# Staging a layer's input in free slots of another operand's tile, and an earlier PSUM read in V

## The chip, the cores and the metric

One core of a Trainium2 chip runs the whole program. The metric is device time in microseconds, the median of three runs. TensorE (PE; its weight loads stand as PEld), VectorE (DVE), ScalarE (ACT), GpSimd (POOL) and the DMA queue of SyncE (SP) work side by side; each engine takes its instructions in order.

## The reference

128 graphs of 128 nodes with 512 features share one adjacency matrix. Layer 0 is a graph convolution, layer 1 attention with 8 heads under the mask of the adjacency; both are pre-normalised and have a residual.

```
h = relu(layernorm(x));  x = x + norm_adj @ (h @ W0) + b0
h = relu(layernorm(x));  q, k, v = h @ Wq + bq, h @ Wk + bk, h @ Wv + bv
attn = softmax(q @ k.T / 8 + (1 - adj) * -1e9)      # 8 heads of 64
x = x + (attn @ v) @ Wo + bo
```

All is float32; x is 128 x 128 x 512.

## The kernel before

The 128 graphs go in 32 groups of four. A group's x stands in two xt tiles (half 0 and half 1, two graphs each, 128 x 1024 float32, 512 KB); the pool has 8 such tiles, so four groups' worth. All five 512 x 512 products of a group are done by a Winograd-like scheme of seven block products P1 to P7; most of these are cut again in the same way. For that an operand tile has 40 slots of 128 x 128: the four blocks A11, A12, S1, A22 (slots 0 to 15), the combinations S2, S3, S4 (16 to 27), and inner combinations (28 to 39). `Operands.combine` (L370) makes the combinations, for most groups on GpSimd: four instructions of 128 x 512 (L373 to L376), then nine of 128 x 256 (L94). There are three such tiles: op_mix (its profile name is op_a) for the graph convolution, op_norm (op_h) for the normalised input of q, k, v, and op_att (op_o) for the output projection.

The program is one software pipeline over slots t. Slot t has five stages, each of seven steps 0 to 6 (a product each): W is the graph convolution's weight product of group t + 1, Q, K and V are q, k, v of group t, and Y is the output projection of group t - 1. `block` (L1092) runs a stage: at each step it first issues whatever is planned for that place, then the step's matmuls and first reads (`step`), then, at the place with a "b", its later reads (`rest`). A place with a "c" comes after both. The list `at(t, place, f, ...)` (L975 and after) is the order written out by hand; no scheduler changes it.

What the later parts speak of, in a slot t:

- `load_x` of group t + 2 at W2 (half 0) and W5 (half 1), from SyncE's queue, L170. It writes an xt tile that held group t - 2, whose `store_half` was issued at the end of Y of slot t - 1 (half 0) or at W3 of slot t (half 1), L903.
- `ln1` (statistics at L325, `bn_stats` on VectorE) at Q0b, Q1b and Q3b; the scale rs and shift nb on GpSimd (L331, L333); `gcn_norm` on ScalarE (L344) at Q3 to Q6; `gcn_mix` on TensorE (bank pa) and ScalarE (L662); `gcn_operands` (op_a) on GpSimd at K2.
- `gcn_residual` adds the bias b0 in place to xt on GpSimd (L348, 128 x 1024) at Y1 and Y2. W of the next slot then adds its products to that xt.
- `norm_h` of group t + 1 on ScalarE (L344) at K6, K6, V0b, V1; `split_h` (L745, 128 x 1024 words in halves) at V0, V0, V1b, V2; `write_h` (L748, DMA to planes_h) at V1b and V2b; `turn_h` (L754, a DMA transpose into op_h) at V5 and Y1b; `attention_operands` (op_h) on GpSimd at Y5.
- the end of attention for group t - 1, in W, Q and K: `softmax_end` (L854, GpSimd), `split_att` (L859, ScalarE; L860, DMA to planes), `turn_att` (L863, DMA transpose), four of each, one per graph b. `attend` (L885, banks po, b and a) reads the result at V0, then `output_operands` combines op_o on GpSimd.
- weights are reloaded from DRAM in four parts (`reload_w`, L1072; 704 KB, the last 448 KB). Into V's buffer go the graph convolution's weights for the next slot: part 0 at V3, part 1 (slots 22 to 32) at Y0, part 2 (slots 11 to 21) at Y1, part 3 at Y3.

In V the seven products write banks a, d0/d1, b and c. V1 fills banks d; ScalarE's copy (L790) moves d0's columns to v, and VectorE (L440) then adds the other parts of d to v; V4 accumulates into banks d again.

Of the kernel before, what the change touches and what calls it, by code (L numbers as in the profile page):

```python
# [8 lines left out]
F32 = mybir.dt.float32  # L9
# [3 lines left out]
ALU = mybir.AluOpType  # L13
# [14 lines left out]
A11, A12, S1, A22, S2, S3, S4 = range(7)  # L28
# [17 lines left out]
LEFT_AT = {A11: 0, A12: 4, S1: 8, A22: 12, S2: 16, S3: 20, S4: 24}  # L46
# [51 lines left out]
def kernel(  # L98
# [16 lines left out]
    nc = tc.nc  # L115
    B, N, D = x.shape
    P = 128
# [10 lines left out]
    xp = ctx.enter_context(tc.tile_pool(name="xp", bufs=8))  # L128
# [32 lines left out]
    ones = att_buf[4][:, NC, :]  # L161
    nc.sync.dma_start(adj_sb, adj)

    xts = {}

    def load_x(g, halves=(0, 1)):
        for half in halves:
            t = xts[g, half] = xp.tile([P, 2, D], F32, tag="xt", name=f"xt_{g}_{half}")
            b = g * GB + 2 * half
            nc.sync.dma_start(t, x[b : b + 2].rearrange("b n f -> n b f"))  # L170

# [30 lines left out]
    def load_b(name, b):  # L202
        t = const.tile([P, D], F32, name=f"b_{name}")
        nc.sync.dma_start(t, b.partition_broadcast(P))
        return t

    xts[0, 0] = xp.tile([P, 2, D], F32, tag="xt", name="xt_0_0")
    for b in range(2):
        nc.sync.dma_start(xts[0, 0][:, b, :], x[b])
    load_w("0", w0, w_buf[0])  # L210
    load_x(0, (1,))
    b0_bc = load_b("0", b0)
    load_x(1)
    load_w("q", wq, w_buf[1])
    bqk = const.tile([P, 2, NC], F32, name="bqk")
# [6 lines left out]
    with nc.allow_non_contiguous_dma(reason="one bias vector, once"):  # L222
        nc.sync.dma_start(bv_c, bv.rearrange("(c p) -> p c", p=P))
    load_x(2)


# [8 lines left out]
    def constants():  # L235
        nc.vector.memset(mhalf, -0.5)
        nc.vector.memset(ones, 1.0)

        nc.scalar.activation(warm, mhalf[:, 0:1], AF.Exp)
        make_identity(nc, ident)  # L240
        nc.gpsimd.tensor_copy(ident16, ident)

        deg = const.tile([P, 1], F32, name="deg")
        nc.vector.tensor_reduce(deg, adj_sb, AX.X, ALU.add)
        degc = const.tile([P, 1], F32, name="degc")
        nc.vector.tensor_scalar(degc, deg, 1.1754944e-38, None, ALU.max)
        dis = const.tile([P, 1], F32, name="dis")
        nc.gpsimd.tensor_tensor(dis, degc, mhalf[:, 0:1], ALU.pow)
        pos = const.tile([P, 1], F32, name="pos")
        nc.vector.tensor_scalar(pos, deg, 0.0, None, ALU.is_gt)  # L250

        nc.vector.tensor_scalar(msk, adj_sb, 1.0, NEG, ALU.subtract, ALU.mult)
        ln1(0, 0, (0,))
        ln1(0, 0, (1,))
        disz = const.tile([P, 1], F32, name="disz")
        nc.vector.tensor_tensor(disz, dis, pos, ALU.mult)
        nc.vector.tensor_scalar(an, adj_sb, disz, None, ALU.mult)
        gcn_norm(0, 0)
        gcn_norm(0, 1)
        spin(9)  # L260
        pt_an = small_bank("pt_an")
        nc.tensor.transpose(pt_an[:, :N], an, ident)
        nc.vector.tensor_scalar(ant, pt_an[:, :N], disz, None, ALU.mult)
# [73 lines left out]
    def normalised(src, j, norm, name, start=False):  # L337
        rs, nb = norm.rs, norm.nb
        if start:

            h = third
        else:
            h = hp.tile([P, D], F32, tag="h", name=name)
        nc.scalar.activation(h, src[:, j, :], AF.Relu, bias=nb[:, j : j + 1], scale=rs[:, j : j + 1])  # L344
        return h

    def add_bias(t, bias):
        nc.gpsimd.tensor_tensor(t, t, bias.unsqueeze(1).to_broadcast([P, t.shape[1], D]), ALU.add)  # L348

# [32 lines left out]
    op_mix, op_norm, op_att = (Operands(f"op_{k}") for k in "aho")  # L384
# [249 lines left out]
    scale1, op_a, op_h, op_o = {}, {}, {}, {}  # L634
    hs = {}

    def ln1(g, half, js=(0, 1), ready=None):

        if (g, half) not in scale1:
            scale1[g, half] = Norm(xts[g, half], f"1_{g}_{half}")  # L640
        for j in js:
            scale1[g, half].statistics(j)
        if ready is None or ready:
            scale1[g, half].scale(ready or js)

    def gcn_norm(g, b):
        half, j = divmod(b, 2)
        hs[g, b] = normalised(xts[g, half], j, scale1[g, half], f"h_{g}_{b}", g == 1 and b == 2)

    def gcn_mix(g, b):  # L650
        if b == 0:
# [14 lines left out]

    def gcn_residual(g, half, js=(0, 1)):

        add_bias(xts[g, half][:, js[0] : js[-1] + 1, :], b0_bc)

    def residual_projection(g, a, w, inner):
        def region(half, y):
# [86 lines left out]
    def attention_residual(g, half):  # L759
        add_bias(xts[g, half], bo_bc)  # L760
# [149 lines left out]
    def at(slot, place, f, *args):  # L910
        plan.setdefault((slot, place), []).append((f, *args))

    for t in range(-1, NG + 1):
# [3 lines left out]
        if 0 <= t - 1 < NG - 1:  # L917
            g = t - 1
# [27 lines left out]
        if t == 0:  # L946

            at(0, "Q0b", ln2, 1, 0)
            at(0, "Q1b", ln2, 1, 1)
            at(0, "K6", norm_h, 1, 0)  # L950
            at(0, "K6", norm_h, 1, 1)
            at(1, "W0", transpose_h, 1, 0)
            at(1, "W0", norm_h, 1, 2)
            at(1, "W1", transpose_h, 1, 1)
            at(1, "W1", norm_h, 1, 3)
            at(1, "W2", transpose_h, 1, 2)
            at(1, "W3", transpose_h, 1, 3)
            at(1, "W4b", attention_operands, 1)
            at(2, "Q5", attention_residual, 1, 0)
            at(2, "K1", attention_residual, 1, 1)  # L960
        elif 1 <= t + 1 < NG and t >= 0:
            g = t + 1
            at(t, "K0b" if g < NG - 1 else "Q0b", ln2, g, 0)
            at(t, "K6b" if g < NG - 1 else "Q3b", ln2, g, 1)
            if g == NG - 1:

                places = ("Q3", "Q4", "Q5", "Q5", "Q6", "Q6", "K1", "K2", "K2")
                steps = ((norm_h, 0), (norm_h, 1), (transpose_h, 0), (norm_h, 2), (transpose_h, 1), (norm_h, 3))
                steps += ((transpose_h, 2), (transpose_h, 3))
            else:  # L970
                places = ("K6", "K6", "V0b", "V1", "V1b", "V2", None, None, "Y5")
                steps = ((norm_h, 0), (norm_h, 1), (norm_h, 2), (norm_h, 3), (split_h, 2), (split_h, 3))
                for half in range(2):
                    at(t, ("V1b", "V2b")[half], write_h, g, half)
                    at(t, ("V5", "Y1b")[half], turn_h, g, half)  # L975
            for place, (f, b) in zip(places, steps):
                at(t, place, f, g, b)
            at(t, places[8], attention_operands, g)
            at(t + 1, "Q3", attention_residual, g, 0)
            at(t + 1, "Q4", attention_residual, g, 1)  # L980
# [1 line left out]

            at(t, "Y3" if t == NG else "Q3" if last else "W3", store_half, t - 2, 1)
        if 3 <= t + 2 < NG:
            at(t, "W2" if t > 1 else "W0", load_x, t + 2, (0,))
            at(t, "W5" if t > 1 else "W0", load_x, t + 2, (1,))
        if 2 <= t + 2 < NG:
            g = t + 2
            if t > 0:
                at(t, "Q0b", ln1, g, 0, (0,), ())  # L990
                at(t, "Q1b", ln1, g, 0, (1,), (0, 1))
                at(t, "Q3b", ln1, g, 1)
            places = (("Q3", "Q5"), ("Q4", "Q6"), ("Q5b", "K1"), ("Q6", "K2"))
            for b, (norm, mix) in enumerate(places):
                at(t, norm, gcn_norm, g, b)
                at(t, mix, gcn_mix, g, b)
            at(t, "K2" if t > 0 else "V1b", gcn_operands, g)
            at(t, "Y1" if t > 0 else "K3", gcn_residual, g, 0)
            at(t, "Y2" if t > 0 else "K3", gcn_residual, g, 1)
        if 0 <= t < NG:  # L1000
            g = t
            for b in (0, 1, 3, 2):
# [31 lines left out]
        if last:  # L1034
            g = t
# [38 lines left out]
    def reloads_of(t):  # L1074

        when = {
            "W": ((t, "W6"), (t, "K3"), (t, "Q1"), (t, "K3")),
            "Q": ((t, "K4"), (t, "K6"), (t, "V0"), (t, "V1")),
            "V": ((t, "V3"), (t, "Y0"), (t, "Y1"), (t, "Y3")),
            "Y": ((t, "Y5"), (t + 1, "W0"), (t + 1, "W0"), (t + 1, "W3" if t + 1 < NG - 1 else "Q5")),  # L1080
        }
        if t == 1:

            when["Q"] = ((1, "K3"),) * 4
        for kind in "WQVY":
            if kind == "W" and t + 1 == NG or kind in "QV" and t == NG:
                continue
            reading[0] += 1
            for part, place in enumerate(when[kind]):
                at(*place, reload_w, reading[0] + 2, part)  # L1090
# [10 lines left out]
    def prologue():  # L1101
# [6 lines left out]
        ln1(0, 1)  # L1108
        combine_w("0", nc.vector, (0, 1, 2))
        gcn_residual(0, 0, (0,))  # L1110
        gcn_norm(0, 2)
        gcn_weight_plain(0)
# [133 lines left out]
```

## Time and profile before

| what | value |
| --- | --- |
| runs | 2233.72, 2235.38, 2240.87 us; median 2235.38 |
| profiled execution | 2238.29 us, of which the span is 2236.5 us |
| TensorE clock granted | 0.998 |
| instructions | 77530 |
| HBM | 358.68 MB read, 137.89 MB written |
| GpSimd: bias adds L348 | 65, 2355 ns each |
| GpSimd: L94 combinations | 732 to 734 ns each |
| VectorE: statistics L325 | 256, 678 ns each |
| ScalarE: normalisation L344 | 254, 818 ns each |
| DMA: x, store of out, h planes | 5.7, 7.2, 3.2 us from issue to landing (median) |

A line of the waits reads: engine, tile and line that waited, then who ended the wait, then the total, the number of times and the longest, in us. A line of the timeline reads: start, busy time, engine, source line, operation, output<-input, shapes, count, and in brackets the engine's idle time ahead of it with what ended it. In the chain of waits a line is start, length and what the time went to. Buffer numbers are left out of names: bank_d is d0 or d1, bank_a is a0 or a1. TensorE's matmul ends are modelled.

### The profile page before, as it was taken

How to read it: one execution, taken by the hardware profiler on the slowest of the kernel's cores; microseconds unless marked ns; L12 is line 12 of the kernel's file. 1: busy time of each engine (PE TensorE's matmuls, PEld its weight loads, DVE VectorE, ACT ScalarE, POOL GpSimd, SP SyncE). 2: the span in 40 equal slices, each digit the busy share in tenths (PEclk: the TensorE clock that was granted, in tenths of full speed). 3: DMA queues.
4: the chain of work that ended last, by engine and by line, in shares of the span. 5: the costliest groups of instructions: out<-in, count | busy, mean ns of one | idle time of the engine just before them, and what ended most of it. 6: DMA issues, size and time to landing. Idle time of an engine off the chain costs nothing.

```text
span 2236.5 us, 77530 instructions
## 1 busy us (share of the span) xinstructions
PE 2205.3 (99%) x31751; PEld 1881.0 (84%) x31751; DVE 1800.5 (81%) x4371; ACT 1385.4 (62%) x3556; POOL 1867.9 (84%) x1928
## 2 busy tenths in 40 slices
PE   9999999999999999999999999999999999999999
PEld 7688888888888888888888888888888888888887
DVE  7777888878878788887788887888887888878876
ACT  4566666665656656666666666566666666665754
POOL 6899888888898888888888988889888888888864
PEclk9999999999999999999999999999999999999999
DMA  5489999999999999999999999999999999999982
GB/s 162 161 268 280 274 276 292 258 280 265 289 281 263 273 304 259 295 277 260 280 284 289 280 264 270 305 267 286 271 269 280 277 287 282 257 282 304 257 255 87
DMA packets 513186, 595.44 MB, mean 266 GB/s; under 512 B 387136, under 2 KB 394432, under 8 KB 512320
## 3 DMA queue, kind: packets, MB, share of 16 engines
q1 hardware_dynamic: 512832, 590.50, 90.4%
q8 instruction: 250, 4.10, 0.7%
q14 instruction: 104, 0.85, 0.1%
HBM read 358.68 MB, written 137.89 MB: 222 GB/s over the span
## 4 chain that ended last, share of the span: by engine, by line
PE 54%; POOL 21%; DVE 9%; DMA 6%; ACT 5%; SPq 3%; issue 3%; DVEq 0%; POOLq 0%
PE bank_a L140 20%; PE bank_d L140 14%; POOL op_a L94 7%; PE bank_c L140 7%; PE bank_b L140 6%; PE pa L140 4%; DMA xt<-in_x_dram 4%; SPq L863 3%; DVE v L440 3%; DVE xt L440 2%; DMA out_dram<-xt 2%; ACT q L745 2%; POOL op_a L376 1%; POOL op_a L374 1%; POOL op_a L373 1%
## 5 line engine op out<-in xcount | busy, mean ns | idle before, releaser
L846 ACT ACTIVATE att<-att,nmx 128x128 f32<-128x128 f32 x1024 | 398.0, 400 | 0.5 <-DVE nmx L838 0.5
L140 PE MATMUL bank_a<-op_h,w 128*64 128x256 f32 x2976 | 352.8, 379 | 0.0
L859 ACT COPY att<-att 128x2048 uint16<-128x2048 uint16 x121 | 229.5, 1897 | 161.7 <-POOL att L854 161.7
L854 POOL TENSOR_TENSOR att<-att,rsm 128x1024 f32<-128x1024 f32 x128 | 241.8, 1899 | 53.2 <-DVE rsm L853 53.2
L440 DVE TENSOR_TENSOR xt<-xt,bank_d 128x512 f32<-128x512 f32 x610 | 270.3, 468 | 11.4 <-PE bank_d L140 0.5
L140 PEld LDWEIGHTS bank_a<-op_h,w 128*64 128x64 f32 x2976 | 207.5, 137 | 81.4 <-issue 0.2
L344 ACT ACTIVATE h<-xt,nb,rs 128x512 f32<-128x512 f32 x254 | 201.3, 818 | 104.5 <-POOL nb L333 102.8
L325 DVE BATCH_NORM_STATS2 st<-xt 128x6 f32<-128x512 f32 x256 | 173.7, 678 | 95.1 <-DMA xt<-in_x_dram 95.1
L331 POOL TENSOR_TENSOR rs<-ve,mhalf 128x2 f32<-128x2 f32 (+1 forms) x129 | 92.0, 713 | 160.8 <-DVE ve L330 159.7
L140 PE MATMUL bank_d<-op_h,w 128*64 128x128 f32 (+1 forms) x3424 | 222.7, 275 | 1.2 <-DVE q L440 0.5
L94 POOL TENSOR_TENSOR op_o<-op_o 128x256 f32<-128x256 f32 x297 | 210.5, 734 | 10.0
L94 POOL TENSOR_TENSOR op_a<-op_a 128x256 f32<-128x256 f32 x279 | 197.6, 732 | 14.4 <-DVE op_a L376 4.8
L140 PEld LDWEIGHTS bank_d<-op_h,w 128*64 128x64 f32 x3424 | 193.8, 137 | 12.0 <-DVE q L440 4.6
L846 ACT ACTIVATION_READ_ACCUMULATOR att<-att,nmx 128x1 f32 x1024 | 203.9, 199 | 0.0
L94 POOL TENSOR_TENSOR op_h<-op_h 128x256 f32<-128x256 f32 x270 | 191.4, 733 | 12.5 <-DVE op_h L376 3.1
L140 PE MATMUL bank_a<-w,op_o 128*64 128x256 f32 x1536 | 182.1, 379 | 0.0
L776 ACT ACTIVATE q<-bank_a,bqk 128x256 f32<-128x256 f32 x192 | 80.1, 468 | 161.7 <-PE bank_a L140 161.7
L140 PE MATMUL bank_a<-w,op_h 128*64 128x256 f32 x1488 | 177.9, 381 | 0.0
L140 PE MATMUL bank_a<-w,op_a 128*64 128x256 f32 x1488 | 176.4, 379 | 0.0
L455 DVE TENSOR_TENSOR xt<-bank_a,xt 128x512 f32<-128x512 f32 x252 | 166.9, 683 | 3.3 <-PE bank_a L140 2.9
L838 DVE TENSOR_REDUCE nmx<-att 128x8 f32<-128x1024 f32 x128 | 155.1, 1212 | 0.0
L348 POOL TENSOR_TENSOR xt<-xt,b 128x1024 f32<-128x1024 f32 (+1 forms) x65 | 152.9, 2355 | 0.0
(183 smaller groups left out, 5611.8 us busy)
## 6 DMA issues: line engine op xcount, KB each, us to landing
w<-wd_v SPq DMA_DIRECT2D x93, 704.0 KB, 5.8
w<-wd_o SPq DMA_DIRECT2D x93, 704.0 KB, 9.0
w<-wd_q SPq DMA_DIRECT2D x90, 704.0 KB, 7.9
planes<-att SPq DMA_DIRECT2D x121, 512.0 KB, 6.4
w<-wd SPq DMA_DIRECT2D x87, 704.0 KB, 5.9
xt<-in_x_dram SPq DMA_DIRECT2D x63, 512.0 KB, 5.7
out_dram<-xt SPq DMA_DIRECT2D x62, 512.0 KB, 7.2
planes_h<-q SPq DMA_DIRECT2D x58, 512.0 KB, 3.2
```

The lines of the kernel that those rows point to most:

```text
L94: engine.tensor_tensor(twice(out), twice(x), twice(y), ALU.subtract if minus else ALU.add)
L140: nc.tensor.matmul(out[y : y + P // 2], lhsT[:, y : y + P // 2], rhs, **flags)
L325: nc.vector.bn_stats(self.st[:, j, :], self.src[:, j, :])
L331: nc.gpsimd.tensor_tensor(self.rs[:, c], self.ve[:, c], mhalf[:, c], ALU.pow)
L344: nc.scalar.activation(h, src[:, j, :], AF.Relu, bias=nb[:, j : j + 1], scale=rs[:, j : j + 1])
L348: nc.gpsimd.tensor_tensor(t, t, bias.unsqueeze(1).to_broadcast([P, t.shape[1], D]), ALU.add)
L440: nc.vector.tensor_tensor(dst, dst, src, f)
L455: nc.vector.tensor_tensor(t, src.rearrange("p (r f) -> p r f", r=2), t, ALU.add)
L838: nc.vector.tensor_reduce(nmx, att_of(g, b), AX.X, ALU.max, negate=True)
L846: nc.scalar.activation(att[:, h, :], att[:, h, :], AF.Exp, bias=nmx[:, h : h + 1], scale=1.0, accum_out=sm[:, h : h + 1])
L854: nc.gpsimd.tensor_tensor(att, att, rsm.unsqueeze(2).to_broadcast([P, H, P]), ALU.mult)
L859: nc.scalar.copy(planes, halves)
```

## The change

For slots t > 1, x of group t + 2 is no longer loaded into an xt tile but into slots of op_o that are free between the end of Y and attention's next output: half 0 into slots 0 to 7 (A11, A12), half 1 into slots 16 to 23 (S2, S3). The loads move from W2 and W5 to W0b and W1. Statistics and normalisation read the staged x. The bias addition reads the staged x and writes the xt tile, which is taken from the pool only there; it moves from Y1 and Y2 to Q6 and K1. In V, the normalisation of graph 3 and the split of graph 2 move to V1c, that is behind ScalarE's copy of d0; the first write of h planes moves from V1b to V1, ahead of the last part of w_o in SyncE's queue. Of the reload of the graph convolution's weights, part 2 is now issued at Y0, and part 1 at Y2, behind the second transpose of h. The order of instructions on TensorE and on VectorE stays as it was.

```diff
-    xts = {}
+    xts, staged = {}, {}
+
+    def source(g, half):
+        return staged.get((g, half)) if (g, half) in staged else xts[g, half]
 
-    def load_x(g, halves=(0, 1)):
+    def load_x(g, halves=(0, 1), stage=False):
         for half in halves:
-            t = xts[g, half] = xp.tile([P, 2, D], F32, tag="xt", name=f"xt_{g}_{half}")
+            if stage:
+                slots = op_att.t[:, (LEFT_AT[A11], LEFT_AT[S2])[half] :][:, :8, :]
+                t = staged[g, half] = slots.rearrange("p (j c) f -> p j (c f)", j=2)
+            else:
+                t = xts[g, half] = xp.tile([P, 2, D], F32, tag="xt", name=f"xt_{g}_{half}")
...
-    def add_bias(t, bias):
-        nc.gpsimd.tensor_tensor(t, t, bias.unsqueeze(1).to_broadcast([P, t.shape[1], D]), ALU.add)
+    def add_bias(t, bias, src=None):
+        src = t if src is None else src
+        nc.gpsimd.tensor_tensor(t, src, bias.unsqueeze(1).to_broadcast([P, t.shape[1], D]), ALU.add)
...
-            scale1[g, half] = Norm(xts[g, half], f"1_{g}_{half}")
+            scale1[g, half] = Norm(source(g, half), f"1_{g}_{half}")
...
-        hs[g, b] = normalised(xts[g, half], j, scale1[g, half], f"h_{g}_{b}", g == 1 and b == 2)
+        hs[g, b] = normalised(source(g, half), j, scale1[g, half], f"h_{g}_{b}", g == 1 and b == 2)
...
-        add_bias(xts[g, half][:, js[0] : js[-1] + 1, :], b0_bc)
+        if (g, half) in staged:
+            t = xts[g, half] = xp.tile([P, 2, D], F32, tag="xt", name=f"xt_{g}_{half}")
+            add_bias(t, b0_bc, staged[g, half])
+        else:
+            add_bias(xts[g, half][:, js[0] : js[-1] + 1, :], b0_bc)
...
-                places = ("K6", "K6", "V0b", "V1", "V1b", "V2", None, None, "Y5")
+                places = ("K6", "K6", "V0b", "V1c", "V1c", "V2", None, None, "Y5")
...
-                    at(t, ("V1b", "V2b")[half], write_h, g, half)
+                    at(t, ("V1", "V2b")[half], write_h, g, half)
...
-            at(t, "W2" if t > 1 else "W0", load_x, t + 2, (0,))
-            at(t, "W5" if t > 1 else "W0", load_x, t + 2, (1,))
+            at(t, "W0b" if t > 1 else "W0", load_x, t + 2, (0,), t > 1)
+            at(t, "W1" if t > 1 else "W0", load_x, t + 2, (1,), t > 1)
...
-            at(t, "Y1" if t > 0 else "K3", gcn_residual, g, 0)
-            at(t, "Y2" if t > 0 else "K3", gcn_residual, g, 1)
+            at(t, "Q6" if t > 1 else "Y1" if t > 0 else "K3", gcn_residual, g, 0)
+            at(t, "K1" if t > 1 else "Y2" if t > 0 else "K3", gcn_residual, g, 1)
...
-            "V": ((t, "V3"), (t, "Y0"), (t, "Y1"), (t, "Y3")),
+            "V": ((t, "V3"), (t, "Y2"), (t, "Y0"), (t, "Y3")),
```

## The prediction

> **What bounds the kernel now.** I read the page's engine rows first, then the waits of TensorE, VectorE and SyncE, then the timeline of one slot (t = 14, Q0 at 1007.9 us), and last the chain of waits in a bad slot (t = 15, Q0 at 1075.8).
>
> ```profile
> PE 2205.3 (99%) x31751; PEld 1881.0 (84%) x31751; DVE 1800.5 (81%) x4371; ACT 1385.4 (62%) x3556; POOL 1867.9 (84%) x1928
> ```
>
> TensorE is the bound, but 99% has modelled matmul ends in it and does not say what is left. That is read from the weight loads, which stop when a bank is not yet free. The waits of PEld, of VectorE and of SyncE's queue (total us, times, longest):
>
> ```profile
> PEld bank_d L140 <- DVE v L440: 11.9, 29, 0.8
> PEld bank_b L140 <- DVE q L440: 8.6, 13, 1.8
> PEld bank_c L140 <- DVE xt L440: 7.6, 10, 1.6
> ...
> PEld bank_d L140 <- DVE q L440: 5.1, 15, 0.7
> ```
> ```profile
> DVE st L325 <- DMA xt<-in_x_dram: 95.1, 57, 3.4
> ```
> ```profile
> SPq L170 <- DMA out_dram<-xt: 94.7, 28, 5.6
> ```
>
> Two troubles. In V, 29 times, bank d is still being read. In Q, VectorE is late with banks b, c and d, and VectorE itself has stood 95.1 us for x. The last line says why x is late: its load (L170) stands in SyncE's queue until the store that frees its xt buffer has landed, 28 times, 3.4 us each. The chain of waits in the bad slot runs from the second half of x to a TensorE stop:
>
> ```profile
> 1082.60 4.76 DMA xt<-in_x_dram
> ...
> 1089.20 1.08 DVE q L440 x3
> 1090.28 0.04 issue
> 1090.32 0.44 PE bank_b L140 x4
> ```
>
> Here TensorE stood 1.57 us ahead of 1090.32. Following Q0 to Q0 through the timeline: slots t = 2 to 29 take 1920.1 us (181.9 to 2102.0), 68.58 each; the best take 67.75, and in those x came at most 2.6 us (half 0) and 9.0 us (half 1) after Q0.
>
> **V: ScalarE's copy ahead of normalisation.** The timeline of V1 to V4:
>
> ```profile
> 1043.89 1.70 PE L140 MATMUL bank_d<-w,op_h 128*64 128x128 f32 x28
> ...
> 1044.65 1.54 ACT L344 ACTIVATE h<-xt,nb,rs 128x512 f32<-128x512 f32 x2
> ...
> 1047.01 0.60 ACT L790 COPY v<-bank_d 128x512 f32<-128x512 f32 x1
> ...
> 1047.64 1.54 DVE L440 TENSOR_TENSOR v<-v,bank_d 128x256 f32<-128x256 f32 x4 [0.64 <-ACT v L790]
> ...
> 1048.02 0.61 PE L140 MATMUL bank_b<-w,op_h 128*64 128x128 f32 x8
> ...
> 1048.78 1.75 PE L140 MATMUL bank_d<-w,op_h 128*64 128x128 f32 x28 [0.16 <-DVE v L440]
> ```
>
> Bank d is full at 43.89 + 1.70 = 1045.59, but ScalarE still does one normalisation (0.82) and one split (1.05), and copies at 1047.01. From bank b to bank d is 0.76 us here; the same step in W is 0.44 (1003.14 to 1003.58). So each slot loses 0.32, and PEld's 0.40 idle overstates that by 0.08. 29 x 0.32 = 9.3 us.
> After: the first normalisation ends near 1045.4, the copy runs 1045.65 to 1046.25, VectorE's reads are bound by its bank b read (1046.58 + 0.42) and start at 1047.0. The read that TensorE needs (the third, 3 x 0.38 on) ends at 1048.17, before the 1048.46 at which TensorE could start. Gain 9.3. Cost: ScalarE idles about 0.2 us, so the second normalisation and the splits end about 0.3 later, and so does the copy of bank a (1049.04 to 1049.34). TensorE wants that bank at 1050.25 - 0.32 = 1049.93: hidden by 0.6 us; uncovered it would cost at most 28 x 0.3 = 8. The exponentials queued behind it have 1.7 us of idle ScalarE ahead of Y. SyncE's write of half 1 waits 0.3 more, in a queue that stands 12 us a slot for just these splits (L748, 373.0 us in all); w_o's last part, now behind the first write, issues at 1044.7 instead of 1033.2 and is wanted in Y6, after 1061.
>
> **Q: x staged early.** The loads no longer need a store to land, and stand in W0b and W1 ahead of planes(1), the other store and w_q's last part. In slot 15 SyncE stood at 1067.8 and issued x half 0 at 1073.29; now both halves issue by 1068. Ahead of them in the DMA engines stand w_q's two parts, landing at 1076.6 (issue plus time to landing). 512 KB landings follow each other by about 1.27 us when the engines are full (planes 1077.9, x 1079.1), so half 0 lands near 1077.9 at worst, half 1 at 1079.1: 2.1 and 3.3 us after Q0, against 3.4 and 11.6. VectorE wants them at 1.2 and 7.3, and best slots show that 2.6 costs TensorE nothing. The Trainium skill, "SBUF — State Buffer" (A bandwidth-pool intuition that's wrong), speaks against a burst like this: HBM gives a core 358 GB/s. By that 512 KB take 1.46 us, by the rows 1.27 (413 GB/s), and half 0 would land 0.8 us later (four transfers, 2.4 MB, ahead of and with it): still about 2.9, a loss of at most some tenths in bad slots. I take the row.
> So I give back the Q waits whole: bank b 8.6 - 13 x 0.08 = 7.6; bank c 7.6 - 0.8 = 6.8; bank d 5.1 - 1.2 = 3.9, less 0.7 of slot 1, which has no x load in Q; the mix (pa) waiting for h 1.1 by PE's own row (PEld's row says 4.5, but a running matmul hides most). Sum 18.7 us.
>
> **What is moved.** Pool's two adds (L348, 2.38 each) leave Y for Q6 and K1. I take 2.38 out of place too; nearest rows 1.90 (L854) and 2.40 (L834), 0.5 less to 0.02 more. The first fills an idle 2.39 us ahead of rs at 1024.98: nothing. The second runs 1026.28 to 1028.66, while op_a's combination would have started at 1027.38: Pool is 1.3 late through K and V. Queued behind it: op_a (wanted 27 us later), rs/nb of the second norm (1040.65 to 1041.9, ScalarE asks at 1045.4), op_o, ending 1052.66 + 1.3 = 1053.96, wanted complete by Y2 at 1056.87 - 0.32: margin 2.6, so nothing; uncovered, each us is 28 us. In Y Pool has 4.8 us less, so op_h starts when its transposed half lands.
> SyncE's swap of two reload parts puts one 704 KB part instead of two ahead of the second transpose of h. The trace shows that a transpose holds the queue until the transfers ahead have landed: issued at 1056.45, it ends at 1063.09, and the part ahead lands at 1063.4. The skill ("DMA: Bandwidth & Descriptors", Rules for kernel authors) says a transpose next to ordinary DMAs needs nothing; by that the swap moves no time, by the row that transpose lands about 3 us earlier. op_h was in time anyway (Q2 finds it 2 us or more ahead), so TensorE gains 0 either way, but W's burst starts with less queued. The part put behind lands near 1065, wanted at W4 near 1071.5: nothing.
>
> **Sum.** 9.3 + 18.7 = 28.0 us. Check: all 28 slots at 67.75 - 0.32 = 67.43 would give 32. Profiled execution 2238.3 (span 2236.5): 2210.3; the median of the runs is 2.9 below it: 2207.4.
>
> **Rivals.** All turn on what is late next: attention's transposes. The one of b = 3 lands (28 slots, issue plus time to landing) 24.1 to 29.8 us after Q0, mean 26.7; an undelayed TensorE asks for it at 27.6. Let d be how much the change delays it.
> (1) Likeliest, d about -1: one half of x more stands ahead of the first transpose (+1.25), but the earlier transpose of h takes up to 2.7 from the queue, and that half is gone from ahead of the second. 2207.4.
> (2) d = 0: late slots that x used to hide now wait here: the excesses over 27.6 sum to 7.8, less 1.3 that po already waits: 6.5 back, 2214. With d = 1.25 it is 21 back: 2228.
> (3) Slower: DMA is the bound (its share of the stretch is 0.96) and the burst delays every transpose by both halves, d = 2.5. The excesses over 27.6 - 2.5 sum to 47, less the 1.3 of now, against 28.0 gained: 2235.4 + 17.7 = 2253. It turns at d = 1.6. Against it: the best slots run at a DMA share of 0.93 to 0.95 and nothing waits there.
> (4) The x part doesn't do what it says (the halves still land 3 us after Q0): V alone, 2235.4 - 9.3 = 2226.
>
> **Chances.** (1) 0.66, within 2201 to 2213; (2) 0.22, two thirds of it near 2214, the rest to 2228; (3) 0.04; (4) 0.05; the last 0.03 some new wait. Range 2201 to 2224. A measurement here tells 0.3% (6.7 us, 2228.7 to 2242.1) from no change: faster 0.89, same 0.07, slower 0.04.
>
> **What would show it.** Right: the wait of DVE st for x gone (under 10 us), SyncE's for out_dram gone at that line, PEld's bank_d <- DVE v near zero, bank_b and bank_c in Q near zero; slots of 67.4 to 67.6; rs ahead of op_a without idle. Wrong: po or bank_d in V waiting for att<-planes (rival 2 or 3); bank_a in V5 waiting for ACT v; bank_b in Y2 waiting for Pool's op_o; st still waiting over 1.5 us (rival 4).

## The result, and the profile after

The changed kernel takes 2208.5 us (median of 2207.73 to 2209.05), the kernel before 2235.36 beside it: ratio 0.9875 (95% interval 0.9858 to 0.9893), 26.9 us faster by the medians and 27.9 by the ratio. The prediction said 2207.4. The profiled execution took 2208.19 us, its span 2206.4.

The page's engine rows of after. Against before, PE has 16.4 us less busy time (modelled matmul ends, stretched by stops); the others differ by at most 5 us.

```profile
PE 2188.9 (99%) x31751; PEld 1880.1 (85%) x31751; DVE 1805.2 (82%) x4371; ACT 1380.6 (63%) x3556; POOL 1868.1 (85%) x1928
```

The waits of after, in the rows that answer to those shown of before (L325 has become L332, L440 L448):

```profile
PEld pa L140 <- ACT h L351: 7.9, 31, 0.9
DVE st L332 <- DMA op_o<-in_x_dram: 7.8, 14, 1.3
...
PEld po L897 <- POOL op_a L94: 3.9, 3, 2.0
...
DVE st L332 <- DMA xt<-in_x_dram: 3.2, 2, 2.5
...
PE po L897 <- DMA att<-planes: 2.0, 2, 1.8
PEld bank_d L140 <- DVE q L448: 1.9, 3, 0.7
```

V's row (bank_d <- DVE v, 11.9 us before) is gone, and with it PEld's rows bank_b <- DVE q and bank_c <- DVE xt. VectorE waits 7.8 us for the staged x and 3.2 for x that still goes to an xt tile, 11.0 in all instead of 95.1. SyncE's wait for the store at the load's line is gone too. What has grown is po, in three slots in which attention's last transpose comes too late. (PEld's row names GpSimd, but PE's own names the transpose att<-planes for two of the three.) Before, that row was:

```profile
PEld po L885 <- POOL op_a L94: 1.4, 3, 0.8
```

V1 to V4 of the same slot (t = 14, Q0 now at 991.9) in the timeline of after:

```profile
1027.78 1.70 PE L140 MATMUL bank_d<-w,op_h 128*64 128x128 f32 x28
...
1029.25 0.59 ACT L802 COPY v<-bank_d 128x512 f32<-128x512 f32 x1
...
1029.72 0.84 ACT L351 ACTIVATE h<-xt,nb,rs 128x512 f32<-128x512 f32 x1
...
1030.80 1.53 DVE L448 TENSOR_TENSOR v<-v,bank_d 128x256 f32<-128x256 f32 x4
1031.91 0.61 PE L140 MATMUL bank_b<-w,op_h 128*64 128x128 f32 x8
...
1032.34 1.70 PE L140 MATMUL bank_d<-w,op_h 128*64 128x128 f32 x28
```

The copy comes 1.47 us after V1 starts (before 3.12), ahead of the normalisation; VectorE starts at 3.02 instead of 3.75; from bank b to bank d TensorE now takes 0.43 us instead of 0.76.

The chain of waits of after, its first row by engine:

```profile
PE 90%; POOL 4%; DMA 2%; DVE 2%; issue 1%; SPq 1%; ACT 1%; DVEq 0%; POOLq 0%; ACTq 0%
```

The same row of before:

```profile
PE 54%; POOL 21%; DVE 9%; DMA 6%; ACT 5%; SPq 3%; issue 3%; DVEq 0%; POOLq 0%
```

Now TensorE ends almost every step last.

Slot by slot (Q0 to Q0, t = 2 to 29) the 28 slots take 1892.9 us, 27.2 less than before. Of those from t = 3 on, 24 of 27 take 67.38 us. The rest of the sum is easy to name: three slots stop ahead of po (t = 7, 9, 15: 0.4, 1.5 and 2.0 us), and t = 2 takes 69.84. With 28 slots of 67.38 the stretch would be 6.3 us shorter: 3.9 of po and 2.5 of t = 2, but for rounding.

In the bad slot t = 15 (Q0 at 1059.3) SyncE's queue and TensorE's po show it:

```profile
1056.58 9.51 SPq L875 DMA_TRANSPOSE att<-planes  x1
...
1066.81 5.92 SPq L875 DMA_TRANSPOSE att<-planes  x1
...
1079.91 4.82 SPq L875 DMA_TRANSPOSE att<-planes  x2
...
1088.85 1.09 PE L897 MATMUL po<-att,v 128*64 128x128 f32 x16 [1.80 <-DMA att<-planes]
```

The second column is the time that a transpose holds the queue: 9.5 us for the first. A hold of that length is usual in this kernel (median 9.7 over the 28 slots); here it ends 6.8 us after Q0, where the median ends at 6.2, and the queue behind it is that much later. The last two issue only from 1079.91 on, and TensorE, having waited 1.80 us, starts on what they bring 29.6 us after Q0.

From here on, landings are means over the 28 slots, in us after a slot's Q0 (issue plus time to landing): x half 0 and half 1, the last transpose of attention (b = 3), and the second transpose of h (counted against the next Q0).

| kernel | x half 0 | x half 1 | attention b = 3 | h, second |
| --- | --- | --- | --- | --- |
| before | 2.67 | 9.56 | 26.71 | −11.18 |
| after | 1.36 | 2.69 | 25.87 | −12.96 |

### The profile page after: what moved, and what is told of

It is laid out like the page before. It is cut to its first block, busy times and chain, and to the rows that moved or that the text cites. A ratio compares the mean times of both kernels' runs of the same rounds, so it can differ in the third digit from the quotient of the medians.

```text
span 2206.4 us, 77557 instructions
## 1 busy us (share of the span) xinstructions
PE 2188.9 (99%) x31751; PEld 1880.1 (85%) x31751; DVE 1805.2 (82%) x4371; ACT 1380.6 (63%) x3556; POOL 1868.1 (85%) x1928
## 4 chain that ended last, share of the span: by engine, by line
PE 90%; POOL 4%; DMA 2%; DVE 2%; issue 1%; SPq 1%; ACT 1%; DVEq 0%; POOLq 0%; ACTq 0%
PE bank_a L140 34%; PE bank_d L140 21%; PE bank_b L140 10%; PE bank_c L140 10%; PE pa L140 5%; PE bank_d L831 3%; PE po L897 2%; PE pss L831 1%; PE bank_b L897 1%; PE bank_a L897 1%; PE bank_b L831 1%; DMA planes<-att 1%; SPq L875 1%; DVE xt L448 1%; DMA att<-planes 1%
## 5 line engine op out<-in xcount | busy, mean ns | idle before, releaser
L448 DVE TENSOR_TENSOR xt<-xt,bank_d 128x512 f32<-128x512 f32 x610 | 270.4, 468 | 11.8 <-DVE xt L448 0.9
L94 POOL TENSOR_TENSOR op_h<-op_h 128x256 f32<-128x256 f32 x270 | 191.2, 733 | 12.4 <-DVE op_h L384 3.1
L858 ACT ACTIVATION_READ_ACCUMULATOR att<-att,nmx 128x1 f32 x1024 | 196.9, 192 | 0.0
L356 POOL TENSOR_TENSOR xt<-xt,b_o 128x1024 f32<-128x1024 f32 x64 | 152.1, 2378 | 0.0
L140 PEld LDWEIGHTS bank_a<-w,op_o 128*64 128x64 f32 x1536 | 107.5, 137 | 41.2
L351 ACT ACTIVATE h<-op_o,nb,rs 128x512 f32<-128x512 f32 x112 | 91.8, 819 | 78.0 <-POOL nb L340 78.0
## 6 DMA issues: line engine op xcount, KB each, us to landing
op_o<-in_x_dram SPq DMA_DIRECT2D x56, 512.0 KB, 10.5
```

The source lines that it names most:

```text
L94: engine.tensor_tensor(twice(out), twice(x), twice(y), ALU.subtract if minus else ALU.add)
L140: nc.tensor.matmul(out[y : y + P // 2], lhsT[:, y : y + P // 2], rhs, **flags)
L356: nc.gpsimd.tensor_tensor(t, src, bias.unsqueeze(1).to_broadcast([P, t.shape[1], D]), ALU.add)
L448: nc.vector.tensor_tensor(dst, dst, src, f)
L858: nc.scalar.activation(att[:, h, :], att[:, h, :], AF.Exp, bias=nmx[:, h : h + 1], scale=1.0, accum_out=sm[:, h : h + 1])
```

## Experiments: which part gives what

My theory was the prediction's sum: V gives 9.3 us, early x gives 18.7, the swap of reload parts nothing. The rivals: that the parts are not additive, and that attention's transposes take part of the gain back. Each time below is a median. The ratio behind it is to runs of the kernel before on the same chip; it is taken over all runs, so it can differ from the ratio of the two medians, by up to 0.001. One us is 0.00045.

**V alone** (kernel before with the V part only).

```diff
-                places = ("K6", "K6", "V0b", "V1", "V1b", "V2", None, None, "Y5")
+                places = ("K6", "K6", "V0b", "V1c", "V1c", "V2", None, None, "Y5")
...
-                    at(t, ("V1b", "V2b")[half], write_h, g, half)
+                    at(t, ("V1", "V2b")[half], write_h, g, half)
```

> The kernel before with only the V part of the change (ScalarE's copy of bank d ahead of the second normalisation, first write of h planes at V1). Theory: the stop between bank b and bank d in V, 0.32 us in 29 slots, goes and the stops in Q stay: 9.3 us, 2226 us. Rival, the two parts hide each other (slots late in Q had slack in V or the other way round): under 4 us, over 2231. A second rival, the later copy of bank a holds up V5: slower than 2235.

2228.24 us, ratio 0.9976 (0.9966 to 0.9986), 5.4 us faster instead of 9.3. The waits of this kernel:

```profile
DVE st L325 <- DMA xt<-in_x_dram: 90.8, 56, 3.6
...
PEld bank_d L140 <- DVE q L440: 8.0, 21, 0.7
```

V's stop is gone, but Q's bank d stops 21 times for 8.0 us (before 15 for 5.1). Banks b and c stop a little less, so that Q's three rows sum to 22.0 (before 21.3), and the row of pa grows from 4.5 to 7.3. So a part of V's gain comes back as stops in Q; how the missing 4 us divide is not shown.

**All but V** (after, with V's part undone: the diff above reversed).

> The changed kernel with the V part undone. Theory: the stops in Q go and the 0.32 us in V stays, so the changed kernel's 2208.5 plus 28 x 0.32 = 9.0: 2217.5 us, and the wait of bank d for DVE v is back at 29 times. Rival, parts not additive: 2208.5 plus 2 to 5, because the wait on attention's transposes (3.8 us in three slots of the changed kernel) is hidden by a slower V.

2217.29 us, 0.9912 (0.9898 to 0.9925). Every steady slot takes 67.74, and TensorE's waits name V again:

```profile
PEld bank_d L140 <- DVE v L448: 11.8, 29, 0.8
```

So on top of the other parts V is worth 67.74 − 67.38 = 0.36 us a slot, 8.2 us by the ratios: near the 9.3.

**Staged, but loaded at the old places.** This parts two things that the change does to x: the tile that it needs no store for, and its place in SyncE's queue.

```diff
-            at(t, "W0b" if t > 1 else "W0", load_x, t + 2, (0,), t > 1)
-            at(t, "W1" if t > 1 else "W0", load_x, t + 2, (1,), t > 1)
+            at(t, "W2" if t > 1 else "W0", load_x, t + 2, (0,), t > 1)
+            at(t, "W5" if t > 1 else "W0", load_x, t + 2, (1,), t > 1)
```

> The changed kernel with x staged as in the change, but loaded at the old places W2 and W5. No store has to land for either load. If the wait for the store was the whole trouble, the time stays within 2 us of 2208.5. Theory: for half 0 it was, but half 1 at W5 stands behind an attention transpose that holds the queue until all ahead has landed (it ends about 6 us after Q0), so half 1 lands near 10.5 against the 7.3 at which it is wanted: VectorE's wait for x is back at 28 times of 2 to 3 us, the stops of bank b in Q come back (7.6 us or more), none for bank c: about 2216 to 2222.

2220.07 us, 0.9925 (0.9912 to 0.9939). The waits of this kernel:

```profile
DVE st L332 <- DMA op_o<-in_x_dram: 89.9, 56, 2.6
...
PEld bank_b L140 <- DVE q L448: 8.4, 17, 1.0
...
PEld bank_d L140 <- DVE q L448: 5.0, 14, 0.8
PEld bank_c L140 <- DVE xt L448: 4.1, 9, 1.1
```

The load waits for no store here: there is no such row of SyncE any more. Yet x lands at 2.63 and 9.42 us after Q0, as before (2.67, 9.56), and VectorE waits 89.9 us for it. In slot t = 14 half 0 is issued 8.48 us ahead of Q0 (before: 3.86) and lands at 2.54 (before: 2.47), each time about 1.2 us behind the landing of the transfer ahead of it, attention's planes (1.31 and 1.22). Half 1 is issued at 4.84 (before: 4.85), when attention's transpose lets go of the queue. The 94.7 us wait for the store was thus no cause of x's lateness: the transfers ahead set the landing of half 0, and the transpose that of half 1. What brings x early is the place: half 0 goes ahead of one 512 KB transfer, and half 1 ahead of attention's transpose, which holds the queue.

**The swap of reload parts undone** (after, with the old order).

```diff
-            "V": ((t, "V3"), (t, "Y2"), (t, "Y0"), (t, "Y3")),
+            "V": ((t, "V3"), (t, "Y0"), (t, "Y1"), (t, "Y3")),
```

> The changed kernel with the order of the two reload parts undone (part 1 at Y0, part 2 at Y1, both ahead of the second transpose of h). By the trace, that transpose then lands 2 to 3 us later, what W issues stands behind it, x half 0 lands about 2 us later after Q0 and attention's last transpose too. From the landings of that transpose in the changed kernel (mean 25.5 us after Q0, wanted at 27.6) a shift of 1.25 costs about 9 us, one of 2.5 about 25: 2217 to 2233. Rival (a transpose needs no regard to other transfers, or the queue catches up before W): within 2 us of 2208.5.

2218.93 us, 0.9916 (0.9903 to 0.9929): 9 us of the gain lost (10.4 by medians), so the swap is no side matter. But not by po, which stops 2.2 us in the profile (after: 3.9). The second transpose of h lands 2.25 us later, and this goes through GpSimd. GpSimd's timeline in one slot:

```profile
1662.93 1.28 POOL L381 TENSOR_TENSOR op_h<-op_h 128x512 f32<-128x512 f32 x1 [3.88 <-DMA op_h<-planes_h]
...
1668.37 6.59 POOL L94 TENSOR_TENSOR op_h<-op_h 128x256 f32<-128x256 f32 x9
1674.91 3.75 POOL L866 TENSOR_TENSOR att<-att,rsm 128x1024 f32<-128x1024 f32 x2
1678.77 0.70 POOL L338 TENSOR_TENSOR rs<-ve,mhalf 128x2 f32<-128x2 f32 x1
```

GpSimd waits 3.88 us for the transpose, so its two att products run until 1674.91 + 3.75 = 1678.66. The timeline of VectorE and TensorE in the same slot:

```profile
1676.95 1.73 DVE L337 TENSOR_SCALAR ve<-mv 128x2 f32<-128x2 f32 x1
1678.60 0.41 DVE L448 TENSOR_TENSOR q<-q,bank_b 128x256 f32<-128x256 f32 x1
...
1679.15 0.66 PE L140 MATMUL bank_b<-op_h,w 128*64 128x128 f32 x8 [0.51 <-DVE q L448]
...
1680.25 1.42 PE L140 MATMUL bank_d<-op_h,w 128*64 128x128 f32 x22 [0.44 <-DVE q L448]
```

`ve` is an addition of 128 x 2 numbers that mostly takes 0.17 us. Here it takes 1.73 and ends when GpSimd's product ends; behind it stand VectorE's reads of banks b and d, and TensorE stops twice. `ve` is held by an att product 17 times (10.1 us in excess of 0.17 each) against 3 times (1.9 us) in after. The other holds, 29 of them behind op_a's combination for 5.3 us, are the same in both kernels. In all, `ve` is held 54 times against 39, and the mean of all 129 is 316 ns against 249.

**Is it the held `ve`?** The old order with this addition on GpSimd, and after with the same.

```diff
-            nc.vector.tensor_scalar(self.ve[:, c], self.mv[:, c, 1], EPS, None, ALU.add)
+            nc.gpsimd.tensor_scalar(self.ve[:, c], self.mv[:, c, 1], EPS, None, ALU.add)
```

> The kernel with the reload order undone, in which the eps addition of every norm (ve, 128 x 2, a TENSOR_SCALAR of VectorE) is done by GpSimd instead. In the reload run ve took up to 1.74 us instead of 0.17, 17 times until the very moment that GpSimd's multiplication of att by rsm (1.9 us) ended, 10.1 us in all. Theory 1 (VectorE's ve is held by GpSimd's instruction, and VectorE then reads banks late): the 10.4 us that undoing the order cost come back, 2207 to 2211. Theory 2 (the later transposes cost it themselves): it stays at 2216 to 2222.

2215.68 us, 0.9911 (0.9892 to 0.9929), not told apart from the old order with `ve` on VectorE. TensorE's row bank_d <- DVE q falls from 7.0 to 1.2 us (PEld), as it should, but another row takes its place:

```profile
PEld pa L140 <- ACT h L351: 19.1, 43, 2.4
```

By PE's own row TensorE now stops 6.4 us there (after: 1.1), because rs and nb come late from GpSimd, and with them the normalised h. So the held `ve` is one of two ways by which GpSimd's lateness reaches TensorE: with it closed, the other takes its place and the time stays.

> The changed kernel with the eps addition on GpSimd. There ve was held 37 times, 10.1 us in all, mostly behind op_a's combination, where nobody waited; TensorE's stops that go with it are 2.2 us in slot 2 and about 1 in slot 1. Theory 1: 2 to 3 us less, 2206. Theory 2: 2208.5 within 1 us; GpSimd has 129 x 0.25 us more to do.

2211.12 us, 0.9892 (0.9873 to 0.9911): the same as after or slightly slower, not the 2206. There is little to save where op_h is early (1.9 us of `ve` behind att products), and the row above has 13.3 us here against 7.9.

**The swap alone** (kernel before, the swap only) and **x alone** (after without V's part and without the swap).

> The kernel before with only the order of the two reload parts changed (part 2 at Y0, part 1 at Y2). The second transpose of h then lands about 2 us earlier. The prediction gave it nothing. Rival: 10 us as measured by undoing it, 2225. In between: before, GpSimd still has the two bias additions in Y and was free for op_h at the transpose's landing in 18 of 30 slots only, so a part of it, 2 to 6 us, 2229 to 2233.

2226.41 us, 0.9955 (0.9939 to 0.9971): 10.1 us from exchanging two transfers. The waits of this kernel:

```profile
DVE st L325 <- DMA xt<-in_x_dram: 79.3, 58, 2.7
...
PEld bank_b L140 <- DVE q L440: 5.1, 12, 1.1
...
PEld bank_d L140 <- DVE q L440: 3.2, 9, 0.7
PEld bank_c L140 <- DVE xt L440: 3.1, 5, 1.1
```

and its SyncE row:

```profile
SPq L170 <- DMA out_dram<-xt: 108.5, 28, 5.9
```

The second transpose of h lands 2.3 us earlier (−13.52), the queue is free sooner, and x lands at 2.28 and 9.09 (at most 3.6 and 10.3, before 4.3 and 11.6). Q's stops for banks b, c and d fall from 21.3 to 11.4 us. The wait for the store even grew, while the kernel became faster: a second sign that it was no cause.

> The change with the V part and the order of the reload parts both undone: only x is staged, loaded at W0b and W1, and the bias additions moved. By the prediction's sum the staging alone is worth 18.7 us: 2216.7, as the V part undone alone gave 2217.3. If what undoing the reload order cost beside the V part (10.4 us, through GpSimd's late start on op_h) is additive, 2208.5 + 8.8 + 10.4 = 2227.7.

2219.64 us, 0.9926 (0.9912 to 0.9939): 16.5 us, near the 18.7 of the prediction's sum; parts that add up would have left 27.9 − 5.4 − 10.1 = 12.4 for x. Most slots take 67.75. GpSimd's own wait in this kernel:

```profile
POOL op_h L381 <- DMA op_h<-planes_h: 37.7, 24, 3.5
```

In after that row has 10.5 us in 12 times, with x and V together (the old order above) 57.5 in 22, with x and the swap 7.6 in 10.

The parts together, in us faster by the ratios (each plus or minus 2 to 4):

| parts | V | swap | x | x + swap | x + V | all |
| --- | --- | --- | --- | --- | --- | --- |
| faster | 5.4 | 10.1 | 16.5 | 19.7 | 18.8 | 27.9 |

x and swap overlap: both cut the Q stops of banks b, c and d, and they give 19.7 where 16.5 + 10.1 would be 26.6. V and swap seem to need each other: on top of x, V gives 2.3; on top of x and swap, 8.2 (each plus or minus 4 to 5, so the times alone do not tell the two apart). The traces point that way. With the shorter V, x + V has the second transpose of h land at −10.71 instead of −11.50, and op_h late is what the swap takes away. The `ve` held by att products follow: before 8 times (2.1 us), V alone 13 (6.3), x 7 (5.1), x + V 17 (10.1); with the swap it is 3 (2.7) alone, 2 (0.8) with x, 3 (1.9) with all.

## Experiments: what could have been late next

**GpSimd's second bias addition three times** (the additions of half 1; the output stays the same). It puts 2 x 2.37 us more in GpSimd's queue at K1, ahead of op_a, rs and op_o.

```diff
-            add_bias(t, b0_bc, staged[g, half])
+            for _ in range(3 if half == 1 else 1):
+                add_bias(t, b0_bc, staged[g, half])
```

> The changed kernel with the bias addition of half 1 at K1 made three times (same operands, same result), 2 x 2.37 us more for GpSimd ahead of op_a, the second norm's scale and op_o. op_o is complete 3.8 us ahead of Y2, and GpSimd then waits for nothing up to there, so TensorE should stop about 0.9 us in Y2 in each of 28 slots, and the second normalisation in V comes as much late: 2234, between 2228 and 2260. Rival (GpSimd has other slack): within 3 us of 2208.5.

2214.44 us, 0.9906 (0.988 to 0.9933). The 25 us that follow from the prediction's deadline, Y2, don't come. The loss has one place, slot t = 2, which takes 76.71 (after 69.84); the steady slots take 67.38 as in after.

```profile
PEld bank_d L140 <- DVE v L448: 3.8, 1, 3.8
```
```profile
224.90 0.81 ACT L351 ACTIVATE h<-xt,nb,rs 128x512 f32<-128x512 f32 x1 [4.97 <-POOL nb L340]
```

In that slot (from 180.6 to 257.3) the second norm's nb stands behind op_a on GpSimd. ScalarE waits 4.97 us for it, its copy of bank d comes behind that normalisation, and TensorE stops in V.

A steady slot of this kernel on GpSimd and TensorE, from its timeline:

```profile
1041.56 6.63 POOL L94 TENSOR_TENSOR op_o<-op_o 128x256 f32<-128x256 f32 x9
```
```profile
1045.30 1.04 PE L140 MATMUL bank_d<-w,op_o 128*64 128x128 f32 x16
...
1047.27 1.04 PE L140 MATMUL bank_b<-w,op_o 128*64 128x128 f32 x16
...
1050.09 0.61 PE L140 MATMUL bank_b<-w,op_o 128*64 128x128 f32 x8
```

op_o is complete at 1048.19, 0.9 us after Y2 started (1047.27), and nobody waits. By the code, Y1 needs the combinations of S1, the first five of these nine (to about 1045.2, so just in time), and the last four are read only in Y4 (1050.09). More than 4.7 us of delay was not tried; it would meet Y1.

**One more load in the burst.** 512 KB of x once more into slots 24 to 31, read by nobody.

```diff
+            if stage and half == 1:
+                more = op_att.t[:, LEFT_AT[S4] :][:, :8, :].rearrange("p (j c) f -> p j (c f)", j=2)
+                nc.sync.dma_start(more, x[b : b + 2].rearrange("b n f -> n b f"))
```

> The changed kernel with one more 512 KB load of x per slot, behind the two staged halves, into slots 24 to 31 of the same tile, read by nobody. It puts every later transfer of the burst back by about 1.27 us and leaves x alone. If attention's last transpose is what is late next, its landings (25.9 us after Q0 in the mean, 29.4 at most, wanted at 27.6) move by 1.27 and the excesses sum to 12.6 instead of 3.9: 9 us slower, 2217, with po as the one that waits. Rival (the queue has slack by then): under 3 us, po as before.

2556.97 us, ratio 1.1437 (1.1411 to 1.1463), for a reason that has nothing to do with the question:

```profile
PE bank_c L140 <- DMA op_o<-in_x_dram: 285.0, 28, 11.5
```

Slot 31 holds an inner block of A22 that the tail of Y still reads in W. This puts the load and TensorE behind one another, and the output projection reads a block that has been overwritten, so this time says nothing on bandwidth. The corrected one loads 448 KB into slots 24 to 30:

```diff
+            if stage and half == 1:
+                more = op_att.t[:, LEFT_AT[S4] :][:, :7, :].rearrange("p s f -> p (s f)")
+                more = more.rearrange("p (j c) -> p j c", j=2)
+                nc.sync.dma_start(more, x[b : b + 2].rearrange("b n f -> n b f")[:, :, 0:448])
```

> The changed kernel with one more load of 448 KB of x per slot behind the two staged halves, into slots 24 to 30 of the same tile, which nobody reads before they are written again (the first try took slot 31 too, which the tail of Y still needs). It puts the later transfers of the burst back by about 1.1 us and leaves x alone. If attention's last transpose is what is late next (landings 25.9 us after Q0 in the mean, 29.4 at most, wanted at 27.6), the excesses grow from 4 to about 11 us: 2215, with po as the one that waits. Rival (slack in the queue): under 3 us.

2210.94 us, 0.9881 (0.9861 to 0.9902), 2.4 us above after, which these runs cannot tell from none. Attention's last transpose lands 0.5 us later (26.36), and po stops 3.5 us in all (after: 3.9). Another 448 KB in every slot costs next to nothing: the burst of x was further from rival 3 than the prediction held.

**Less ahead of attention's transposes.** Part 0 of the reload into W's buffer is moved from W6 to K3, so that it no longer stands ahead of them.

```diff
-            "W": ((t, "W6"), (t, "K3"), (t, "Q1"), (t, "K3")),
+            "W": ((t, "K3"), (t, "K3"), (t, "Q1"), (t, "K3")),
```

> The changed kernel with part 0 of the reload of w_v moved from W6 to K3, so that nothing stands between the first two transposes of attention. If the queue sets when attention's last transpose lands, it lands 1 to 2 us earlier, po's stops (3.8 us in the changed kernel's profile) go, and the time is 2204 to 2206. Rival (ScalarE's splits set it, or the later reload is late for V): 2208.5 or slower.

2219.13 us, 0.9922 (0.9909 to 0.9935), not the 2204 to 2206. The edit has a fault: part 0 is what turns the weight's name from the tile of its first load to the buffer, and part 2 (at Q1) is now issued ahead of it. In slot t = 1 the name still means op_o's tile, so part 2 lands there, and the kernel's output is wrong. In that slot there is one long stop:

```profile
PEld pa L140 <- ACT h L351: 19.8, 30, 12.8
```

That slot takes 84.45 us instead of 70.97, which is more than the whole loss. In the other slots what was expected is there: the last transpose lands 2.4 us earlier (mean 23.48, at most 25.4), po no longer stops, and the slots t = 2 to 29 take 1888.9 us, 4.0 less than in after. So the queue's order sets that landing, and the 3.9 us of po look recoverable; as the total is worse and the output wrong, a kernel that beats after was not shown.

## Why the prediction was right, and where its steps were not

- **V, 9.3 us: right as part of the whole** (alone it gave 5.4). 0.33 less from bank b to bank d in the slot shown, 0.36 a slot where all else is equal, 8.2 us by the ratios. The later copy of bank a is hidden, as said: no row of waits names it.
- **Q, 18.7 us: right in size** (x alone 16.5; with all three, VectorE's wait for x went from 95.1 to 11.0 us, and Q's stops for banks b, c and d from 21.3 to 1.9). x lands at 2.0 and 3.3 us in slot 15 (foreseen: 2.1 and 3.3), at most 2.5 and 3.8 over all slots. The 358 GB/s of the Trainium skill ("SBUF — State Buffer", A bandwidth-pool intuition that's wrong) asked for 0.8 us more (0.9, for the 2.4 MB that the prediction names), and that did not come. In after the two halves land 1.33 us apart in the mean (1.29 in slot 15), nearer the row's 1.27 than the 1.46 by that rule.
- **"The last line says why x is late": wrong.** The load did stand in the queue until the store had landed, but with that wait taken away and the place kept, x lands where it did. A wait in an in-order queue names what ended last, not what sets the landing. The sum held because the change moves the place too.
- **The swap, "TensorE gains 0 either way": wrong.** The transposed half lands 1.8 us earlier (2.3 by the swap alone; the prediction said about 3), so the row told the way it went. The sentence of the Trainium skill ("DMA: Bandwidth & Descriptors", Rules for kernel authors) stands beside a warning on corrupted results and says nothing of time; the prediction read too much into it. But I looked for the swap's worth only at op_h's first reader, Q2. It lies with what stands behind op_h on GpSimd (att products, rs, nb) and behind the transpose in SyncE's queue (x). Alone it gives 10.1 us. The 28.0 was made of V and Q, and these came to that size only with the swap. That the swap was in the change was, for the sum, luck: without it the same sum would have stood, and x + V measured 18.8.
- **GpSimd "1.3 late through K and V": did not happen.** The second addition begins 16.8 us after Q0, not 18.4 as I had placed it, because rs comes earlier with x (15.6 instead of 17.1). Its rows in the timeline of after:

```profile
1008.73 2.37 POOL L356 TENSOR_TENSOR xt<-op_o,b 128x1024 f32<-128x1024 f32 x1
...
1011.26 1.27 POOL L381 TENSOR_TENSOR op_a<-op_a 128x512 f32<-128x512 f32 x1 [0.16 <-ACT op_a L670]
```

  op_a starts 19.4 us after Q0, before 19.5; the 2.37 us for the addition was right.
- **"Wanted complete by Y2 … margin 2.6 … each us is 28 us": wrong**, and harmless here. The readers are Y1 for the first part and Y4 for the last; 4.7 us more of GpSimd's work cost no steady slot anything. It was slot t = 2 that paid, by the second norm's nb and not by op_o.
- **Attention's transposes, d about −1: right.** The mean landing moved from 26.71 to 25.87, −0.84. The working was only in part right: x alone, without the earlier transpose of h, gives −0.78, so it did not take the earlier transpose of h to make up for the half of x put ahead. The excess over 27.6, in three slots, is 3.4 us (po's row has 3.9), between rival 1 (none) and rival 2 (6.5). Rival 3 did not come near even with 448 KB more a slot.
- **The sum.** 28.0 foreseen, 26.9 measured. The check (all slots alike) said 67.43 and 32 us; the slots are 67.38, and 6.3 us are lost to po and to slot t = 2; the reckoning had not looked at that slot by itself. In it PEld stops 0.7 us each at q's banks b and d, behind a `ve` of 1.51 us, and 1.8 us at pa, as in the kernel before. That the slot would gain without the held `ve` is not shown: with `ve` on GpSimd it takes 70.66.

What stays open: why `ve` on GpSimd doesn't gain the 2 us that it frees (the runs are no finer than that), and how the 10 us of the swap divide between the x landing and GpSimd when x is late.

## What to carry to other kernels

A wait in an in-order queue shows what came last; before a gain is put down to its removal, ask which transfers stand ahead, and whether the place in the queue or the wait decides. Take the parts of a change one by one and in pairs: here an edit counted at nothing was worth 10 us alone and seems to have decided what another edit was worth. And read a deadline from the first instruction that reads each piece, not from the stage that uses the tile; then follow the late engine to everything that is queued behind that piece.

## What the runs showed of the hardware that was not expected

- A tiny VectorE instruction can be held for as long as a GpSimd instruction lasts: the 128 x 2 TENSOR_SCALAR took 0.17 us mostly and up to 1.74, ending with GpSimd's TENSOR_TENSOR. All 54 held ones in the kernel with the old order end 23 to 31 ns after such an instruction does. This agrees with the Trainium skill, "SBUF — State Buffer" (Who interferes with whom): a `tensor_scalar` whose operands allow it may enter a mode that takes a port pair shared with GpSimd, and then one of the two "fully blocks". That it is this mode, no run here shows. On VectorE all that stands behind it in order pays too, here the reads of PSUM banks.
- A DMA transpose holds SyncE's queue (9.51 us in the slot shown) while other transfers are under way; over the 148 that had plain transfers ahead in the kernel before, it let go 0.19 us ahead of the last one's landing in the median. So one part of a weight reload ahead of it or behind it moved its landing by 1.8 to 2.3 us, and with it what came after in that queue.
